# Pairwise bilinear products on one core: one ring of PSUM banks and multiplies of up to 2048 columns

## The chip, the cores and the metric

The kernel runs on one core of a Trainium2 chip. The metric is the device time of one execution in microseconds. The kernel before takes 1341.25 us (median of three executions, 1340.96 to 1341.39). The profiled execution has a span of 1339.7 us from its first to its last instruction.

## What is computed

The input x has 4096 rows of 32 fields with 64 numbers each, in float32. For each of the 496 pairs of fields (i, j) with i < j there is a 64 x 64 matrix W. The output for a pair is the row vector x_i times W, multiplied element by element with x_j:

```python
i_idx, j_idx = np.triu_indices(32, k=1)        # 496 pairs, i < j
vi = inputs[:, i_idx, :]                       # (4096, 496, 64)
vj = inputs[:, j_idx, :]
vdotw = jnp.einsum('bpd,pde->bpe', vi, W)
inter = vdotw * vj
return inter.reshape(B, -1)                    # (4096, 31744)
```

The output is 4096 x 31744 float32, 520 MB. Input x is 33.6 MB and W is 8.1 MB (8.4 MB with the zeros that the host adds).

## The kernel before

A row tile is 128 rows; there are 32. For a field i, all its products with later fields lie side by side in the output, (31 - i) x 64 columns wide. The kernel takes two fields at a time, 2p and 2p + 1, which it calls a pair p (16 of them): field 2p of x, transposed, lies on partitions 0 to 63 and field 2p + 1 on partitions 64 to 127, and so do their weights. The two halves of a pair differ by 64 columns in width; the host pads the weights of the second half with 64 zeros, so both have equal width in SBUF.

For each chunk of 512 columns, two matmuls (one per half) fill the two banks of one PSUM tile of 1024 columns, and VectorE multiplies the result with columns of x and writes it into a ring of 28160 columns in SBUF. When both halves of the chunk are 512 wide, one instruction multiplies both (1024 columns, read as two runs); the last chunk of a pair, where the halves differ, takes one instruction per half. PSUM has eight banks of 512 float32 columns; the kernel has them as four buffers of two banks.

```python
P = 128
BANK = 512
STORES = [[0, 1], [2, 3], [4, 5], [6, 7, 8], [9, 10, 11, 12, 13, 14, 15]]
PREFETCH_AT = [5, 6]
RING = 28160
...
psum = ctx.enter_context(tc.tile_pool(name="ps", bufs=4, space=bass.MemoryType.PSUM))
...
for t in range(NT):
    xt, xT = xs.pop(t), xTs.pop(t)
    if t + 1 < NT:
        xs[t + 1] = load_x(t + 1)
    for s, group in enumerate(STORES):
        ...                                    # osb: the next store_w[s] columns of the ring
        for p in group:
            if t + 1 < NT and p in PREFETCH_AT:
                ...
                transpose_x(xTs[t + 1], t + 1, xs[t + 1], PREFETCH_AT.index(p))
            for c0 in range(0, width[2 * p], BANK):
                pm = psum.tile([P, 2, BANK], F32, tag="ps", name=f"pm_{t}_{p}_{c0}")
                n = [max(0, min(BANK, width[2 * p + h] - c0)) for h in range(2)]
                for h in range(2):
                    if n[h]:
                        nc.tensor.matmul(pm[:, h, : n[h]],
                                         xT[h * D : (h + 1) * D, ts(p, P)],
                                         w_sb[p][h * D : (h + 1) * D, c0 : c0 + n[h]],
                                         start=True, stop=True)      # L120
                ...
                if n[0] == n[1]:
                    nc.vector.tensor_tensor(runs(osb, o[0], o[1], n[0]),
                                            pm[:, :, : n[0]],
                                            runs(xt, xj[0], xj[1], n[0]), ALU.mult)   # L130
                else:
                    for h in range(2):
                        if n[h]:
                            nc.vector.tensor_tensor(...)             # L139, one half each
        nc.sync.dma_start(out=out[ts(t, P), o0 : o0 + store_w[s]], in_=osb)   # L145
```

`transpose_x` takes one more PSUM buffer of the same four: eight 128 x 128 transposes on TensorE (L80), then a copy by ScalarE to SBUF (L81). It runs twice per row tile, ahead of pairs 5 and 6, for the next row tile. The pairs of one group in STORES are written to HBM with one transfer when the group is done; there are five such stores per row tile, of 2.75 to 3.78 MB (2752 to 3776 KB).

Of the kernel before, what the change touches and what calls it, by code (L numbers as in the profile page):

```python
# [1 line left out]

# [6 lines left out]

F32 = mybir.dt.float32  # L10
ALU = mybir.AluOpType

P = 128
BANK = 512

STORES = [[0, 1], [2, 3], [4, 5], [6, 7, 8], [9, 10, 11, 12, 13, 14, 15]]
PREFETCH_AT = [5, 6]
RING = 28160


@with_exitstack
def pair_bilinear_kernel(
    ctx: ExitStack,
    tc: tile.TileContext,
    x: bass.AP,
    w: bass.AP,
    out: bass.AP,
    F: int,
    D: int,
):  # L30

    nc = tc.nc
    B = x.shape[0]
    NT = B // P
    NPR = F // 2  # L50

    width = [(F - 1 - i) * D for i in range(F)]
    off = [sum(width[:i]) for i in range(F)]
    woff = [sum(width[0 : 2 * p : 2]) for p in range(NPR)]
    store_w = [sum(width[2 * p] + width[2 * p + 1] for p in g) for g in STORES]

    const = ctx.enter_context(tc.tile_pool(name="const", bufs=1))
    xpool = ctx.enter_context(tc.tile_pool(name="x", bufs=2))
    xtpool = ctx.enter_context(tc.tile_pool(name="xT", bufs=2))
    psum = ctx.enter_context(tc.tile_pool(name="ps", bufs=4, space=bass.MemoryType.PSUM))  # L60

    ident = const.tile([P, P], F32, tag="ident", name="ident")
    make_identity(nc, ident)

    def runs(tl, a, b, n):

        ap = tl[:, a : a + n]
        return bass.AP(ap.tensor, ap.offset, [list(ap.ap[0]), [b - a, 2], list(ap.ap[1])])

    def load_x(t):  # L70
        xt = xpool.tile([P, F * D], F32, tag="x", name=f"x_{t}")
        nc.scalar.dma_start(out=xt, in_=x[ts(t, P), :])
        return xt

    def transpose_x(xT, t, xt, g):

        n = 2 * BANK // P
        pt = psum.tile([P, 2 * BANK], F32, tag="ps", name=f"pt_{t}_{g}")
        for c in range(n):
            nc.tensor.transpose(pt[:, ts(c, P)], xt[:, ts(n * g + c, P)], ident)  # L80
        nc.scalar.copy(xT[:, ts(g, 2 * BANK)], pt)  # L81

    def new_xT(t):
        return xtpool.tile([P, NPR * P], F32, tag="xT", name=f"xT_{t}")

    ring = const.tile([P, RING], F32, tag="ring", name="ring")
    at = 0
    xs = {0: load_x(0)}

    w_sb = []  # L90
    for p in range(NPR):
        wp = const.tile([P, width[2 * p]], F32, tag=f"w{p}", name=f"w{p}")
        nc.sync.dma_start(out=wp, in_=w[:, woff[p] : woff[p] + width[2 * p]])
        w_sb.append(wp)

    xTs = {0: new_xT(0)}
    for g in range(2):
        transpose_x(xTs[0], 0, xs[0], g)
# [6 lines that stand above are left out]
            if at + store_w[s] > RING:  # L105
                at = 0
            osb = ring[:, at : at + store_w[s]]
            at += store_w[s]
            o0 = off[2 * group[0]]
            for p in group:  # L110
                if t + 1 < NT and p in PREFETCH_AT:
                    if t + 1 not in xTs:
                        xTs[t + 1] = new_xT(t + 1)
                    transpose_x(xTs[t + 1], t + 1, xs[t + 1], PREFETCH_AT.index(p))
                for c0 in range(0, width[2 * p], BANK):
                    pm = psum.tile([P, 2, BANK], F32, tag="ps", name=f"pm_{t}_{p}_{c0}")
                    n = [max(0, min(BANK, width[2 * p + h] - c0)) for h in range(2)]
                    for h in range(2):
                        if n[h]:
                            nc.tensor.matmul(  # L120
                                pm[:, h, : n[h]],
                                xT[h * D : (h + 1) * D, ts(p, P)],
                                w_sb[p][h * D : (h + 1) * D, c0 : c0 + n[h]],
                                start=True,
                                stop=True,
                            )
                    o = [off[2 * p + h] - o0 + c0 for h in range(2)]
                    xj = [(2 * p + h + 1) * D + c0 for h in range(2)]
                    if n[0] == n[1]:
                        nc.vector.tensor_tensor(  # L130
                            runs(osb, o[0], o[1], n[0]),
                            pm[:, :, : n[0]],
                            runs(xt, xj[0], xj[1], n[0]),
                            ALU.mult,
                        )
                    else:
                        for h in range(2):
                            if n[h]:
                                nc.vector.tensor_tensor(  # L139
                                    osb[:, o[h] : o[h] + n[h]],  # L140
                                    pm[:, h, : n[h]],
                                    xt[:, xj[h] : xj[h] + n[h]],
                                    ALU.mult,
                                )
            nc.sync.dma_start(out=out[ts(t, P), o0 : o0 + store_w[s]], in_=osb)  # L145


# [33 lines left out]
```

## Time and profile before

| what | value |
|---|---|
| time, median of three | 1341.25 us |
| span of the profiled execution | 1339.7 us |
| mean granted TensorE clock | 0.949 |
| HBM read / written | 41.94 MB / 520.09 MB |
| multiplies of 1024 columns (L130) | 768, mean 1217 ns |
| multiplies of one half, 64 to 448 columns (L139) | 896, mean 415 ns |
| matmul records of the products (L120) | 4864, mean 559 ns |
| transposes (L80), copies of them (L81) | 512, mean 297 ns; 64, mean 1012 ns |
| a store, from issue to landing | 22 to 23 us |

In the profile, PE is TensorE's matmuls, PEld its loads of weights (which overlap the matmuls), DVE is VectorE, ACT is ScalarE, SP issues the stores. A group of instructions is given as line, engine, operation, output<-input by the program's names (partitions x elements) and count, then the busy time in us and the mean duration in ns, then the time for which the engine stood idle before them and what ended that wait. Busy time is the time that a group covers; where two instructions overlap, it counts once, so it can be less than count times mean. In the row of slices, each digit is the busy share of a fortieth of the span in tenths, 9 being 90% or more. A line in the list of DMA queues has packets, megabytes, and the share of the 16 DMA engines' time. Matmuls are pipelined and their ends are modelled, so the busy share of PE does not say how near it is to its peak.

### The profile page before, as it was taken

The numbers are of one execution on the slowest core, as the hardware profiler recorded it, in microseconds if no ns is written. First come the engines' busy times: TensorE is split into PE (matmuls) and PEld (weight loads), VectorE is DVE, ScalarE is ACT, GpSimd is POOL, SyncE is SP. The second block draws the span as 40 slices with busy tenths as digits, with TensorE's granted clock in tenths as the row PEclk, the third lists the DMA queues.
The fourth block names the chain that finished last, engine by engine and source line by source line (L and its number), as shares of the span: only waits on it lengthen the run. The fifth ranks groups of instructions, "written<-read, shape, count | busy, mean of one in ns | idle before, by whom it ended". The sixth has DMA issues, their size and how long they took to land.

```text
span 1339.7 us, 13755 instructions
## 1 busy us (share of the span) xinstructions
PE 1151.0 (86%) x5376; PEld 548.7 (41%) x5376; DVE 1177.4 (88%) x1664; ACT 66.1 (5%) x65; POOL 0.7 (0%) x6
## 2 busy tenths in 40 slices
PE   7998889888898888988888978889798897888992
PEld 3444344443343443443433534444344443444441
DVE  6999889888899988989888989899898997898993
ACT  1000000000000000000000000000000000000000
POOL 0000000000000000000000000000000000000000
PEclk9999889999999999989999899899898998998996
DMA  9999999999999999999999999999999999999996
GB/s 392 426 431 434 429 431 429 427 427 434 426 434 430 422 422 430 422 424 429 415 426 424 426 426 404 415 420 431 428 420 408 431 427 431 416 424 420 422 429 264
DMA packets 30017, 562.93 MB, mean 420 GB/s; under 512 B 3456, under 2 KB 3840, under 8 KB 5376
## 3 DMA queue, kind: packets, MB, share of 16 engines
q1 hardware_dynamic: 25344, 528.49, 92.6%
q10 hardware_dynamic: 4608, 33.56, 6.0%
q8 instruction: 42, 0.69, 0.2%
q14 instruction: 23, 0.19, 0.0%
HBM read 41.94 MB, written 520.09 MB: 420 GB/s over the span
## 4 chain that ended last, share of the span: by engine, by line
DMA 54%; DVE 23%; PE 11%; issue 9%; DVEq 0%
DMA out_dram<-ring 54%; DVE ring L130 15%; PE pm L120 9%; DVE ring L139 9%; PE pt L80 2%; DMA x<-in_x_dram 1%; DVEq L130 0%; DVEq L177 0%
## 5 line engine op out<-in xcount | busy, mean ns | idle before, releaser
L120 PE MATMUL pm<-w,xT 64*128 64x512 f32 (+7 forms) x4864 | 1083.2, 559 | 158.3 <-DVE ring L130 140.1
L130 DVE TENSOR_TENSOR ring<-pm,x 128x1024 f32<-128x1024 f32 x768 | 904.0, 1217 | 138.4 <-DMA out_dram<-ring 93.0
L120 PEld LDWEIGHTS pm<-w,xT 64*128 64x128 f32 x4864 | 487.7, 194 | 720.1 <-DVE ring L130 451.3
L139 DVE TENSOR_TENSOR ring<-pm,x 128x448 f32<-128x448 f32 (+6 forms) x896 | 330.2, 415 | 3.6 <-PE pm L120 2.9
L81 ACT COPY xT<-pt 128x1024 f32<-128x1024 f32 x64 | 64.8, 1012 | 1194.6 <-PE pt L80 1194.6
L80 PE MATMUL pt<-ident,x 128*128 128x128 f32 x512 | 76.5, 297 | 8.5 <-DMA x<-in_x_dram 8.5
L80 PEld LDWEIGHTS pt<-ident,x 128*128 128x128 f32 x512 | 61.0, 152 | 48.9 <-issue 35.3
L81 ACT ACT_TABLE_LOAD x1 | 1.3, 1283 | 1.7 <-PEq L173 1.7
masks.py:199 POOL TENSOR_SCALAR_AFFINE_SELECT ident<-ident 128x128 f32<-128x128 f32 x1 | 0.3, 292 | 0.1
masks.py:197 POOL MEMSET ident<- 128x128 f32 x1 | 0.2, 204 | 0.3 <-POOLq L173 0.3
L173 POOL MEMSET const-bfloat16-1.0<- 128x1 bf16 x1 | 0.1, 101 | 0.0
L173 POOL MEMSET const-uint8-127<- 128x1 uint8 x1 | 0.1, 101 | 0.0
L173 POOL MEMSET const-float32-0.0<- 128x1 f32 x1 | 0.1, 98 | 0.2 <-issue 0.2
L173 POOL MEMSET const-float32-1.0<- 128x1 f32 x1 | 0.1, 98 | 0.0
## 6 DMA issues: line engine op xcount, KB each, us to landing
out_dram<-ring SPq DMA_DIRECT2D x32, 3776.0 KB, 22.8
out_dram<-ring SPq DMA_DIRECT2D x32, 3264.0 KB, 21.8
out_dram<-ring SPq DMA_DIRECT2D x32, 3168.0 KB, 22.4
out_dram<-ring SPq DMA_DIRECT2D x32, 2912.0 KB, 22.3
out_dram<-ring SPq DMA_DIRECT2D x32, 2752.0 KB, 22.1
x<-in_x_dram ACTq DMA_DIRECT2D x32, 1024.0 KB, 14.2
w<-in_w_dram SPq DMA_DIRECT2D x1, 992.0 KB, 7.4
w<-in_w_dram SPq DMA_DIRECT2D x1, 928.0 KB, 11.7
```

The costliest lines, as they stand in the source:

```text
L80: nc.tensor.transpose(pt[:, ts(c, P)], xt[:, ts(n * g + c, P)], ident)
L81: nc.scalar.copy(xT[:, ts(g, 2 * BANK)], pt)
L120: nc.tensor.matmul(pm[:, h, : n[h]], xT[h * D : (h + 1) * D, ts(p, P)], w_sb[p][h * D : (h + 1) * D, c0 : c0 + n[h]], start=True, stop=True,)
L130: nc.vector.tensor_tensor(runs(osb, o[0], o[1], n[0]), pm[:, :, : n[0]], runs(xt, xj[0], xj[1], n[0]), ALU.mult,)
L139: nc.vector.tensor_tensor(osb[:, o[h] : o[h] + n[h]], pm[:, h, : n[h]], xt[:, xj[h] : xj[h] + n[h]], ALU.mult,)
L173: nc = bacc.Bacc("TRN2", target_bir_lowering=False, num_devices=1)
```

## The change

PSUM becomes one tile of eight banks, and a small allocator hands out banks in turn; a request that doesn't fit before the end starts again at bank 0. A chunk is up to 1024 columns of each half: when the first half has more than 512 columns left, the chunk takes four banks, two per half, and otherwise two banks. One VectorE instruction multiplies both halves of a chunk, up to 2048 columns.

Unequal halves are also done in one instruction, both with the width of the first. The second half then gets 64 columns more than it has. The matmul fills them with zeros, because the weights there are zeros; the columns of x read for them run up to 64 columns past the end of a row, so x lies in two fixed buffers with 64 zero columns behind it; and the 64 products of zero are written beyond the pair's own place in the ring, where the next pair of the group writes its own values afterwards. That can't be done for the last pair of a group, nor where the second half doesn't reach into the chunk's last bank; those still take one instruction per half.

The purpose is fewer, longer VectorE instructions. The diff, with comments and blank lines left out:

```diff
+BANKS = 8
+CHUNK = 2 * BANK
...
-    xpool = ctx.enter_context(tc.tile_pool(name="x", bufs=2))
-    psum = ctx.enter_context(tc.tile_pool(name="ps", bufs=4, space=bass.MemoryType.PSUM))
+    psum = ctx.enter_context(tc.tile_pool(name="ps", bufs=1, space=bass.MemoryType.PSUM))
...
+    xbuf = [const.tile([P, (F + 1) * D], F32, tag=f"x{b}", name=f"x{b}") for b in range(2)]
+    for xb in xbuf:
+        nc.gpsimd.memset(xb[:, F * D :], 0.0)
...
+    pring = psum.tile([P, BANKS * BANK], F32, tag="pring", name="pring")
+    bank = 0
+    def take_banks(n):
+        nonlocal bank
+        if bank + n > BANKS:
+            bank = 0
+        got = pring[:, bank * BANK : (bank + n) * BANK]
+        bank = (bank + n) % BANKS
+        return got
...
-        pt = psum.tile([P, 2 * BANK], F32, tag="ps", name=f"pt_{t}_{g}")
+        pt = take_banks(2)
...
-                for c0 in range(0, width[2 * p], BANK):
-                    pm = psum.tile([P, 2, BANK], F32, tag="ps", name=f"pm_{t}_{p}_{c0}")
-                    n = [max(0, min(BANK, width[2 * p + h] - c0)) for h in range(2)]
-                    for h in range(2):
-                        if n[h]:
-                            nc.tensor.matmul(pm[:, h, : n[h]], ...)
+                for c0 in range(0, width[2 * p], CHUNK):
+                    n = [max(0, min(CHUNK, width[2 * p + h] - c0)) for h in range(2)]
+                    half = -(-n[0] // BANK) * BANK
+                    pm = take_banks(2 * half // BANK)
+                    for b0 in range(0, n[0], BANK):
+                        b1 = min(b0 + BANK, n[0])
+                        for h in range(2):
+                            if b0 < n[h]:
+                                nc.tensor.matmul(pm[:, h * half + b0 : h * half + b1], ...)
...
-                    if n[0] == n[1]:
+                    if n[1] > half - BANK and o[1] + n[0] <= store_w[s]:
                         nc.vector.tensor_tensor(
                             runs(osb, o[0], o[1], n[0]),
-                            pm[:, :, : n[0]],
+                            runs(pm, 0, half, n[0]),
                             runs(xt, xj[0], xj[1], n[0]),
                             ALU.mult,
                         )
```

More of the change, by code (lines that the diff above doesn't have):

```diff
@@ L68, in runs @@
         return bass.AP(ap.tensor, ap.offset, [list(ap.ap[0]), [b - a, 2], list(ap.ap[1])])
+    xbuf = [const.tile([P, (F + 1) * D], F32, tag=f"x{b}", name=f"x{b}") for b in range(2)]
+    for xb in xbuf:
+        nc.gpsimd.memset(xb[:, F * D :], 0.0)
     def load_x(t):
-        xt = xpool.tile([P, F * D], F32, tag="x", name=f"x_{t}")
-        nc.scalar.dma_start(out=xt, in_=x[ts(t, P), :])
-        return xt
+        xt = xbuf[t % 2]
+        nc.scalar.dma_start(out=xt[:, : F * D], in_=x[ts(t, P), :])
+        return xt
+    pring = psum.tile([P, BANKS * BANK], F32, tag="pring", name="pring")
[7 more added lines that the diff above has]
+        return got
     def transpose_x(xT, t, xt, g):
         n = 2 * BANK // P
-        pt = psum.tile([P, 2 * BANK], F32, tag="ps", name=f"pt_{t}_{g}")
+        pt = take_banks(2)
         for c in range(n):
@@ L114, in pair_bilinear_kernel @@
                     transpose_x(xTs[t + 1], t + 1, xs[t + 1], PREFETCH_AT.index(p))
-                for c0 in range(0, width[2 * p], BANK):
-                    pm = psum.tile([P, 2, BANK], F32, tag="ps", name=f"pm_{t}_{p}_{c0}")
-                    n = [max(0, min(BANK, width[2 * p + h] - c0)) for h in range(2)]
-                    for h in range(2):
-                        if n[h]:
[L120 to L126, printed above, removed]
+                for c0 in range(0, width[2 * p], CHUNK):
[6 more added lines that the diff above has]
+                            if b0 < n[h]:
+                                nc.tensor.matmul(
+                                    pm[:, h * half + b0 : h * half + b1],
+                                    xT[h * D : (h + 1) * D, ts(p, P)],
+                                    w_sb[p][h * D : (h + 1) * D, c0 + b0 : c0 + b1],
+                                    start=True,
+                                    stop=True,
+                                )
                     o = [off[2 * p + h] - o0 + c0 for h in range(2)]
                     xj = [(2 * p + h + 1) * D + c0 for h in range(2)]
-                    if n[0] == n[1]:
+                    if n[1] > half - BANK and o[1] + n[0] <= store_w[s]:
                         nc.vector.tensor_tensor(
                             runs(osb, o[0], o[1], n[0]),
-                            pm[:, :, : n[0]],
+                            runs(pm, 0, half, n[0]),
                             runs(xt, xj[0], xj[1], n[0]),
@@ L140, in pair_bilinear_kernel @@
                                     osb[:, o[h] : o[h] + n[h]],
-                                    pm[:, h, : n[h]],
+                                    pm[:, h * half : h * half + n[h]],
                                     xt[:, xj[h] : xj[h] + n[h]],
```

## The prediction

> **What bounds the kernel now.** I read the page's totals and its row of DMA shares first, then the groups by shape, then the waits of VectorE, and last the timeline of a few microseconds. The totals and the DMA part of the page:
>
> ```profile
> PE 1151.0 (86%) x5376; PEld 548.7 (41%) x5376; DVE 1177.4 (88%) x1664; ACT 66.1 (5%) x65; POOL 0.7 (0%) x6
> DMA  9999999999999999999999999999999999999996
> DMA packets 30017, 562.93 MB, mean 420 GB/s; under 512 B 3456, under 2 KB 3840, under 8 KB 5376
> q1 hardware_dynamic: 25344, 528.49, 92.6%
> q10 hardware_dynamic: 4608, 33.56, 6.0%
> ```
>
> Neither TensorE nor VectorE is full, but the transfers are: 92.6% for weights and stores plus 6.0% for the loads of x is 98.6% of the span, and no slice but the last falls under nine tenths. So the DMA engines set the pace: 0.986 x 1339.7 = 1321 us over 32 row tiles is **41.3 us a tile**. The waits say the same from the other side (engine, line waited for: total us, times, longest):
>
> ```profile
> DVE ring L130 <- DMA out_dram<-ring: 93.0, 53, 3.3
> DVE ring L130 <- PE pm L120: 45.4, 52, 13.2
> ```
>
> VectorE waits 93.0 us for space in the output ring, that is, for stores to land. For TensorE it waits 45.4 us, of which 13.2 is the start. Its time adds up: 1177.4 busy + 93.0 + 45.4 + 2.9 (the same wait at L139) = 1319 us, and its last multiply ends at 1319.5. Without the ring wait it would need (1177.4 + 32.2 + 2.9) / 32 = **37.9 us a tile**. So the producer has only 3.4 us a tile in hand.
>
> **What one multiply costs.** From the groups by shape:
>
> ```profile
> L130 DVE TENSOR_TENSOR ring<-pm,x 128x1024 f32<-128x1024 f32 x768 | 904.0, 1217 | 138.4 <-DMA out_dram<-ring 93.0 <-PE pm L120 45.4
> L139 DVE TENSOR_TENSOR ring<-pm,x 128x448 f32<-128x448 f32 x128 | 78.9, 617 | 3.6 <-PE pm L120 2.9
> L139 DVE TENSOR_TENSOR ring<-pm,x 128x64 f32<-128x64 f32 x128 | 27.6, 215 | 0.0
> ```
>
> (1217 - 617) / (1024 - 448) = 1.042 ns a column, or 960 columns a microsecond, and about 150 ns fixed. Back to back, neighbours overlap by some 0.085 us. What remains fixed is the busy time less the columns: 1177.4 / 32 = 36.79 us a tile, 31744 columns take 33.07, and 52 instructions share the other 3.72: **0.072 us each**.
>
> **What one refill of PSUM costs.** This decides my prediction. The timeline (start, length):
>
> ```profile
> 224.83 3.48 DVE L130 TENSOR_TENSOR ring<-pm,x 128x1024 f32<-128x1024 f32 x3
> 228.36 0.30 PEld L120 LDWEIGHTS pm<-w,xT 64*128 64x128 f32 x4 [0.83 <-DVE ring L130]
> ...
> 233.80 7.97 PE L120 MATMUL pm<-w,xT 64*128 64x512 f32 x38
> ...
> 234.34 0.19 PEld L120 LDWEIGHTS pm<-w,xT 64*128 64x128 f32 x2 [0.24 <-issue]
> 234.76 0.19 PEld L120 LDWEIGHTS pm<-w,xT 64*128 64x128 f32 x2 [0.23 <-issue]
> 234.98 2.36 DVE L130 TENSOR_TENSOR ring<-pm,x 128x1024 f32<-128x1024 f32 x2 [0.29 <-PE pm L120]
> ```
>
> A multiply ends at 224.83 + 3.48 = 228.31 and TensorE begins on the bank it freed at 228.36: 0.05 us. The lower lines show a multiply that waited: matmuls begin at 233.80, it starts at 234.98, **1.18 us** later, with two banks filled. The page counts 4864 matmul records, 152 a tile, where the loops call 76, so a call is two records. Loads of weights come in pairs every 0.43 us, so the two calls that fill two banks take 0.86 us, and 0.32 us is the way from matmul to multiply. Four banks then take 1.72 + 0.32 = 2.04 us, and from bank freed to multiply started it is **2.09 us**.
>
> [...]
>
> **The change, part by part.** *Multiplies.* Walking the loops, a tile goes from 52 multiplies over 31744 columns to 29 over 32320: nine unequal pairs are merged and each writes 64 extra zeros. 32320 / 960 + 29 x 0.072 = 33.67 + 2.09 = 35.75 us, so **1.0 us a tile is saved**. Since VectorE already waits 93 us for stores, this alone is hidden. *Matmuls* stay at 76 calls; transposes, loads, stores and bytes don't change. The two memsets at the start are outside the path.
>
> *Buffers.* Before: four slots of two banks, so TensorE may be three slots ahead. After: a chunk over 512 columns a half takes four banks, and only two such chunks fit. A refill can begin only when the multiply two chunks back has ended, and has one multiply as cover. A multiply of 2048 lasts 2.205 us in sequence and just covers 2.09. A short one doesn't. With the ring's order of banks worked out by hand, wrap included, the stall is 2.09 + 0.085 less the sequence time of the work between. In one tile:
>
> | chunk that stalls (columns) | work that covers it | its time | stall us |
> |---|---|---|---|
> | pair 0, first (2048) | pairs 14, 15: 384 + 64 | 0.61 | 1.56 |
> | pair 1, first (2048) | 1920 | 2.07 | 0.10 |
> | pair 2, first (2048) | 832 + 768 | 1.81 | 0.36 |
> | pair 3, first (2048) | 1408 | 1.54 | 0.64 |
> | pair 4, first (2048) | 576 + 512 | 1.28 | 0.90 |
> | pair 5, first (2048) | 896 | 1.00 | 1.17 |
> | pair 6, first (2048) | 320 + 256 | 0.74 | 1.43 |
> | pair 7, first (2048) | 384 | 0.47 | 1.70 |
> | pair 8 (1856, refill 1.98) | 64 | 0.14 | 1.93 |
>
> Pairs 6 to 8 stand in it because banks 6 and 7 are skipped when four no longer fit before the end, or hold a transpose. The later pairs find cover. The sum is **9.8 us a tile** in place of some 1.1 now. Then VectorE needs 35.75 + 9.8 = **45.5 us a tile**, more than the 41.3 of the DMA engines: the producer becomes the bound and the 93 us of ring waits vanish. The mean granted clock is 0.949; at that, nine refills of 1.72 us grow by 0.09 each and the tile takes 46.4.
>
> *The sum.* The first multiply starts at 13.16 now, and 0.86 later with four banks to fill: 14.0. Then 32 tiles: 1457 us at full clock, 1484 at 0.949, less 1.6 as the first tile has no tile before it. After the last multiply the program now takes 1339.7 - 1319.5 = 20.2 us; I keep 20. The measured time is 1.5 over the span. That is 14 + 1457 - 1.6 + 20 + 1.5 = 1491 us, or about 1518 at the lower clock. I take **1505 us**.
>
> **Rivals.** *Hidden by the transfers, 1341 us.* If refills overlapped better than my table has it, so that the stalls stay under 41.3 - 35.75 = 5.5 us a tile, the DMA engines stay the bound. For it: the full DMA row, and that TensorE's own work, 31 x 0.86 + 2 x 1.02 = 28.7 us a tile, is far under the limit. Against it: the table would have to be nearly twice too high, and its terms are seen in the trace. *The saving reaches the end.* If VectorE were the bound all along, 32 x 1.0 = 33 us go and 1308 us remain. The 93 us of ring waits and 420 GB/s speak against it. *A wait of VectorE on itself.* The 64 zeros that a merged multiply writes past its end are overwritten by the next pair's multiply; should that one be made to wait for the former's end, it loses the 0.085 us of overlap and some signalling, perhaps 0.12 us in six places a tile that no stall covers: 0.7 us a tile, 1528 us. Nothing in this trace shows whether it is made to wait.
>
> **Range and chances.** The low end takes a third off the stalls: 45.5 - 3.3 = 42.2 us a tile gives 1386, but a quarter off is as much as I believe, 43.1 or 1415. The high end is the lower clock with the wait on itself, 1541, and a little. So 1415 to 1545. Slower by over 2% gets 0.88, within 2% 0.09 for the hiding rival, faster 0.03.
>
> **What would show it.** VectorE's busy time falls from 1177 to about 1144 us with 928 multiplies. Its waits for TensorE rise from 48 to some 310 us in about nine places a tile, and its waits for stores fall from 93 to near zero. The DMA row loses its nines, with about 563 / 1.5 = 375 GB/s. A multiply that follows a lone 64-column one starts nearly 2 us late. If the waits for stores stay and the DMA row is full, the stall table is wrong and the first rival holds. A granted clock far from 0.949 would move the sum by some 27 us either way.

## The result, and the profile after

The changed kernel takes 1523.87 us (median, 1520.22 to 1526.17), the kernel before 1341.35 us measured beside it: a ratio of **1.136** (95% interval 1.134 to 1.138). The prediction was 1505 us in a range of 1415 to 1545.

The totals of the page after, with its rows for the TensorE clock and the transfers:

```profile
PE 1218.4 (80%) x5376; PEld 575.6 (38%) x5376; DVE 1176.2 (77%) x928; ACT 66.1 (4%) x65; POOL 0.9 (0%) x8
PEclk9999999999999999999999999999999999999998
DMA  9988898888988889888889888898888988889977
q1 hardware_dynamic: 25344, 528.49, 82.0%
```

The bytes are the same, but the DMA engines now have gaps in most slices: 82.0% in place of 92.6% for the stores and weights. VectorE runs 928 instructions in place of 1664 and is busy for as long as before. The waits after (engine, line waited for: us in total, times, longest):

```profile
DVE ring L155 <- PE pring L145: 239.5, 229, 15.2
DVE ring L164 <- PE pring L145: 83.5, 32, 3.5
```

No wait of VectorE for a store is left. It now waits for TensorE, 323 us in all, where before it was 48. The producer, TensorE and VectorE together, has become the bound. The timeline of VectorE shows where: the end of one row tile (pairs 7 to 10), then pairs 0 to 7 of the next (start, length; the number in brackets is the wait):

```profile
418.47 2.29 DVE L155 TENSOR_TENSOR ring<-pring,x 128x2048 f32<-128x2048 f32 x1 [1.63 <-PE pring L145]
420.68 0.21 DVE L164 TENSOR_TENSOR ring<-pring,x 128x64 f32<-128x64 f32 x1
422.73 2.16 DVE L164 TENSOR_TENSOR ring<-pring,x 128x960 f32<-128x960 f32 x2 [1.83 <-PE pring L145]
424.80 3.61 DVE L155 TENSOR_TENSOR ring<-pring,x 128x1664 f32<-128x1664 f32 x2
...
433.67 6.75 DVE L155 TENSOR_TENSOR ring<-pring,x 128x2048 f32<-128x2048 f32 x3 [1.08 <-PE pring L145]
440.34 1.88 DVE L164 TENSOR_TENSOR ring<-pring,x 128x832 f32<-128x832 f32 x2
442.51 3.82 DVE L155 TENSOR_TENSOR ring<-pring,x 128x2048 f32<-128x2048 f32 x2 [0.29 <-PE pring L145]
446.89 2.29 DVE L155 TENSOR_TENSOR ring<-pring,x 128x2048 f32<-128x2048 f32 x1 [0.56 <-PE pring L145]
...
451.27 3.29 DVE L155 TENSOR_TENSOR ring<-pring,x 128x2048 f32<-128x2048 f32 x2 [0.83 <-PE pring L145]
455.65 2.29 DVE L155 TENSOR_TENSOR ring<-pring,x 128x2048 f32<-128x2048 f32 x1 [1.09 <-PE pring L145]
457.86 0.81 DVE L164 TENSOR_TENSOR ring<-pring,x 128x320 f32<-128x320 f32 x2
460.04 2.76 DVE L155 TENSOR_TENSOR ring<-pring,x 128x2048 f32<-128x2048 f32 x2 [1.36 <-PE pring L145]
464.42 2.29 DVE L155 TENSOR_TENSOR ring<-pring,x 128x2048 f32<-128x2048 f32 x1 [1.62 <-PE pring L145]
```

Read it as a staircase. From pair 2 to pair 7 the wait ahead of the first chunk is 0.29, 0.56, 0.83, 1.09, 1.36 and 1.62 us; each cover, the second chunk of the pair before, takes 0.27 us less than the last (1.81, 1.54, 1.28, 1.00, 0.74 and 0.47 us in the prediction's table). Pair 8, covered only by 64 columns, waits 1.83. The table in the prediction had 0.36, 0.64, 0.90, 1.17, 1.43, 1.70 and 1.93, counted from where the multiply would have started with the usual overlap of 0.085 us; less that overlap the two agree within 0.02 us. These are waits at the full clock; what a lower clock adds is told below.

### The profile page after: what moved, and what is told of

The parts are those of the page before. It is cut to its first block, busy times and chain, and to the rows that moved or that the text cites. A ratio compares the mean times of both kernels' runs of the same rounds, so it can differ in the third digit from the quotient of the medians.

```text
span 1524.4 us, 12666 instructions
## 1 busy us (share of the span) xinstructions
PE 1218.4 (80%) x5376; PEld 575.6 (38%) x5376; DVE 1176.2 (77%) x928; ACT 66.1 (4%) x65; POOL 0.9 (0%) x8
## 4 chain that ended last, share of the span: by engine, by line
DVE 55%; PE 41%; issue 3%; DMA 0%; DVEq 0%
DVE ring L155 51%; PE pring L145 41%; DVE ring L164 4%; DMA x<-in_x_dram 0%; PE pring L102 0%; DVEq L155 0%; DVEq L164 0%
## 5 line engine op out<-in xcount | busy, mean ns | idle before, releaser
L145 PE MATMUL pring<-w,xT 64*128 64x512 f32 (+4 forms) x4864 | 1146.7, 559 | 286.2 <-DVE ring L155 277.0
L155 DVE TENSOR_TENSOR ring<-pring,x 128x2048 f32<-128x2048 f32 (+6 forms) x544 | 939.6, 1747 | 252.2 <-PE pring L145 239.5
L145 PEld LDWEIGHTS pring<-w,xT 64*128 64x128 f32 x4864 | 519.7, 192 | 893.2 <-DVE ring L155 462.5
L164 DVE TENSOR_TENSOR ring<-pring,x 128x64 f32<-128x64 f32 (+8 forms) x384 | 255.3, 700 | 86.8 <-PE pring L145 83.5
L103 ACT COPY xT<-pring 128x1024 f32<-128x1024 f32 x64 | 64.8, 1012 | 1377.7 <-PE pring L102 1336.7
L102 PE MATMUL pring<-ident,x 128*128 128x128 f32 x512 | 78.2, 287 | 8.4 <-DMA x<-in_x_dram 8.4
L102 PEld LDWEIGHTS pring<-ident,x 128*128 128x128 f32 x512 | 55.8, 143 | 44.3 <-issue 42.2
```

Of the source, the lines that this page charges most:

```text
L145: nc.tensor.matmul(pm[:, h * half + b0 : h * half + b1], xT[h * D : (h + 1) * D, ts(p, P)], w_sb[p][h * D : (h + 1) * D, c0 + b0 : c0 + b1 ...
L155: nc.vector.tensor_tensor(runs(osb, o[0], o[1], n[0]), runs(pm, 0, half, n[0]), runs(xt, xj[0], xj[1], n[0]), ALU.mult,)
L164: nc.vector.tensor_tensor(osb[:, o[h] : o[h] + n[h]], pm[:, h * half : h * half + n[h]], xt[:, xj[h] : xj[h] + n[h]], ALU.mult,)
```

## The experiments

**Two-bank chunks with everything else changed.** The merging of unequal halves and the ring of banks stay; only the chunk goes back to 512 columns a half.

```diff
-CHUNK = 2 * BANK
+CHUNK = BANK
```

> The changed kernel with chunks of 512 columns a half again, so every chunk takes two banks; the ring of banks and the merging of unequal halves stay. Theory (too few chunks fit in PSUM to cover a refill): a refill now has three chunks of cover, 43 multiplies take 32320 / 960 + 43 x 0.072 = 36.8 us a tile, some 1.7 more for the nine places where VectorE waits for itself and 1.1 for TensorE make 39.6, under the 41.3 of the DMA engines: 1341 us, and the waits for stores come back. Rival (the merging with its waits of VectorE on itself is the loss): the nine places are all still there, so the time stays near 1524. Rival (the ring of banks as one tile ties the engines together): also near 1524.

Measured: 1339.58 us, a ratio to the kernel before of 0.9988 (0.9982 to 0.9995). In its waits the stores are back, and TensorE is nearly gone (13.9 of the 32.0 us is the start):

```profile
DVE ring L155 <- DMA out_dram<-ring: 53.4, 35, 2.9
DVE ring L155 <- PE pring L145: 32.0, 29, 13.9
```

So neither the ring as one tile nor the merging is enough to make the kernel slower; what they may cost stays hidden under the transfers. The four-bank chunks are needed for the loss.

**Long chunks only where a long multiply covers them, and only where none does.** In both, the changed kernel's chunk depends on the pair:

```diff
-                for c0 in range(0, width[2 * p], CHUNK):
+                chunk = CHUNK if p < 4 else BANK              # second kernel: 4 <= p <= 8
+                for c0 in range(0, width[2 * p], chunk):
```

> The changed kernel with chunks of 1024 a half only in pairs 0 to 3, where a long multiply follows to cover the refill, and 512 a half from pair 4 on. Theory of PSUM cover: of the stalls in the table only those of pairs 0 to 3 remain, 1.1 + 0.1 + 0.4 + 0.6 = 2.2 us; 36.3 for the multiplies and some 1.5 for self-waits make 40 us a tile, just under the 41.3 of the DMA engines: 1341 to 1350 us. Rival (any multiply over four banks is slow, wherever it stands): four of the eight long ones remain, so about half the loss, 1430 us.

> The other half: chunks of 1024 a half only in pairs 4 to 8, where short multiplies follow, and 512 a half elsewhere. Theory of PSUM cover: the stalls of pairs 4 to 8 remain, about 0.9 + 1.2 + 1.4 + 1.7 + 1.9 = 7.1 us, 36.4 for the multiplies, some 1 for self-waits and 0.9 for the slow clock: 45 us a tile, 1470 us (1440 to 1510). Rival (any multiply over four banks is slow): half the loss, 1430 us, the same as with the early pairs.

Measured: 1339.06 us with the long chunks in pairs 0 to 3 (ratio 0.9984, 0.9977 to 0.9991), and 1424.17 us with them in pairs 4 to 8 (1.0619, 1.0603 to 1.0635). The waits of the first, then of the second:

```profile
DVE ring L156 <- PE pring L146: 86.3, 128, 13.9
DVE ring L156 <- DMA out_dram<-ring: 13.8, 18, 2.2
```

```profile
DVE ring L156 <- PE pring L146: 148.1, 131, 13.7
DVE ring L165 <- PE pring L146: 55.9, 32, 2.9
```

Taken alone, the 1424 us are below the theory's range and close to the rival's 1430. What decides is the pair of runs: the early pairs have eight four-bank chunks a row tile and the late ones five, yet only the late ones lose. So a multiply over four banks is not slow in itself. With the early pairs VectorE still waits for TensorE, 2.3 us a row tile without the start, (86.3 - 13.9) / 32, as the table had it (2.2); that fits under the time of the transfers, for which it goes on waiting. The late pairs cost less than expected, 43.7 us a row tile in place of 45: pair 7 waited 0.89 us instead of 1.62, because the trace has a multiply of 640 columns, of a later pair, between it and pair 6 (more on that below), pair 8 waited 1.71 instead of 1.83, and the clock stayed high (0.995).

**Fewer buffers, multiplies as they were.** The kernel before, with two buffers of two banks.

```diff
-    psum = ctx.enter_context(tc.tile_pool(name="ps", bufs=4, space=bass.MemoryType.PSUM))
+    psum = ctx.enter_context(tc.tile_pool(name="ps", bufs=2, space=bass.MemoryType.PSUM))
```

> The kernel before with two PSUM buffers of two banks in place of four; instructions, stores and loads are unchanged. Theory of PSUM cover: a refill of two banks takes 1.23 us and has one multiply of 1.14 or less as cover; the same table, chunk by chunk, gives 13.6 us of stalls a tile on 36.8 of multiplies: 50.4 us a tile, 13 + 32 x 50.4 + 10 = about 1640 us, with the multiplies as short as ever. Rival (it is the long multiplies that cost, not the number of buffers): 1341, as the DMA engines would still be the bound.

Measured: 1652.45 us, one run, where about 1640 was expected. Its row tiles take 51.0 us (31 periods between first multiplies), where the table worked out for it gave 50.4. The waits:

```profile
DVE ring L130 <- PE pm L120: 355.7, 418, 13.4
DVE ring L139 <- PE pm L120: 47.5, 51, 1.8
```

No instruction changed, and VectorE waits 403 us for TensorE. So fewer buffers in flight are enough for such a loss, and long multiplies are not needed for it.

**Half of the output not stored.** Each store writes only the first half of its columns, in the kernel before and in the changed one, so half of the output is left out and half of the store traffic is gone. The edit does a little more than that: a store no longer needs the multiplies of its second half, so it goes out earlier, and VectorE need not wait to overwrite that half.

```diff
-            nc.sync.dma_start(out=out[ts(t, P), o0 : o0 + store_w[s]], in_=osb)
+            nc.sync.dma_start(out=out[ts(t, P), o0 : o0 + store_w[s] // 2], in_=osb[:, : store_w[s] // 2])
```

> The kernel before, but each store writes only the first half of its columns: half of the output is left out, all multiplies stay. Theory (before, the DMA engines are the bound and VectorE has 3.4 us a tile in hand): the ring waits vanish and the time falls to VectorE's own 37.9 us a tile: 13 + 32 x 37.9 + 12 = 1238 us. Rival (VectorE or TensorE was the bound already): near 1341.

> The changed kernel, with the same half of the output left out. Theory (the producer is the bound, the transfers are not): the time stays at 1524, less 2 to 4 us as the last store is shorter. Rival (the transfers are still part of the loss, for instance because they run slower): it falls by 50 us or more.

Measured, one run each: 1194.73 us for the kernel before, where 1238 was expected, and 1512.28 us for the changed one. The totals of the first:

```profile
PE 1100.7 (92%) x5376; PEld 519.4 (44%) x5376; DVE 1168.4 (98%) x1664; ACT 66.1 (6%) x65; POOL 0.7 (0%) x6
```

VectorE is full at 98%. A row tile takes 36.81 us: 36.51 in which its 52 multiplies keep VectorE busy and one wait of 0.29 for TensorE. So the transfers were the bound before, and the producer had 4.5 us a tile in hand, not the 3.4 of the prediction. Of the 1.1 us of waits for TensorE that I had counted as its own, 0.29 remain. TensorE's clock is at 1.00 in this run and was 0.949 before; whether that is the reason is not shown.

The changed kernel loses only 12 us when half its stores go (14 between the two traced executions, with spans of 1524.4 and 1510.5 us). 7.7 of the 14 lie after the last multiply, 1.5 us in place of 9.2, where 2 to 4 were expected: the last store needs only pairs 9 and 10, and goes out 4.2 us before the last multiply ends. Row tiles take 46.66 in place of 46.85, which is 6 us over the run; up to the last multiply there are 17 stretches at half clock in place of 22. The first multiply starts 1 us earlier. The transfers are no longer the bound.

**Unequal halves not merged.** Chunks up to 1024 columns a half stay.

```diff
-                    if n[1] > half - BANK and o[1] + n[0] <= store_w[s]:
+                    if n[0] == n[1]:
```

> The changed kernel with chunks of up to 1024 columns a half, but unequal halves always take one multiply each, so no multiply writes past its place and none has to wait for the one before. Theory of PSUM cover: the nine refills stay uncovered; 31744 / 960 + 38 x 0.072 = 35.8 us a tile, 9.4 of stalls, no self-waits, and 0.9 for the slow stretches of TensorE's clock: 46.1 against 46.85 us a tile, 1500 us. Rival (self-waits and zeros are the loss): back to 1341 to 1380.

Measured: 1436.46 us (1.0713, 1.0697 to 1.0729). It lies between the two expectations, and neither has the size: long chunks without merging still cost 95 us over the kernel before, and the merging costs another 87 on top, not 24. The trace gives three parts of the 2.78 us a row tile (46.85 to 44.07). First the self-waits. Groups of the changed kernel by shape, then of this one:

```profile
L155 DVE TENSOR_TENSOR ring<-pring,x 128x640 f32<-128x640 f32 x32 | 26.4, 825 | 3.3
```

```profile
L164 DVE TENSOR_TENSOR ring<-pring,x 128x640 f32<-128x640 f32 x64 | 52.1, 815 | 0.0
```

In the changed kernel VectorE stands idle 3.3 / 32 = 0.10 us ahead of this multiply with no engine named. What the trace has there is a wait for a semaphore that VectorE's own multiplies raise; the multiply before it wrote zeros into its place. Without merging it starts 0.085 us before its neighbour ends. That is 0.19 us in each of four places (pairs 10, 13, 14 and 15), and 0.08 ahead of pair 1's first chunk: 0.8 us. Second, the clock: it stayed high here (0.997, no stretch at half clock before the last multiply), and in the changed kernel row tiles without such a stretch take 45.95 us, 0.9 under the mean. Third, about 1.1 us net, the order: with single halves the compiled program has moved multiplies of pairs 9 and 11 ahead, between the short ones of pairs 6 and 7. The timeline of VectorE shows it as three multiplies where pair 6 has two, and two where pair 7 has one:

```profile
616.28 1.41 DVE L164 TENSOR_TENSOR ring<-pring,x 128x192 f32<-128x192 f32 x3
618.45 2.29 DVE L155 TENSOR_TENSOR ring<-pring,x 128x2048 f32<-128x2048 f32 x1 [0.76 <-PE pring L145]
620.66 0.81 DVE L164 TENSOR_TENSOR ring<-pring,x 128x64 f32<-128x64 f32 x2
622.71 3.09 DVE L164 TENSOR_TENSOR ring<-pring,x 128x960 f32<-128x960 f32 x3 [1.24 <-PE pring L145]
```

The waits of pairs 7 and 8 fall from 1.62 and 1.83 to 0.76 and 1.24; 0.30 us come back as a wait in pair 10. More cover, less wait: the same mechanism again, from a side that the expectation had not thought of.

**Work for TensorE while it waits.** Redundant matmuls, overwritten by the real ones:

```diff
+                        if p in (6, 7) and c0:
+                            for h in range(2):
+                                if n[h]:
+                                    nc.tensor.matmul(pm[:, h * half : h * half + BANK], xT[...], w_sb[p][..., :BANK], ...)
```

> The changed kernel with redundant matmuls of 512 columns ahead of the second chunks of pairs 6 and 7, into the same banks, overwritten by the real ones; they fill time in which TensorE waits for a bank anyway. Theory (some 23 stretches of half clock, most of them at pair 8 after TensorE has been idle much, cost 0.9 us a tile of the loss): fewer such stretches and the tile goes from 46.85 towards the 45.95 of the tiles without one, 1495 to 1510 us. Rival (the half clock falls at fixed times or for another reason, or costs nothing): 1524, or later by the added matmuls, up to 1550.

Measured: 1498.78 us, 25 us less than the changed kernel (1.1175, 1.1157 to 1.1194, over the kernel before; the changed kernel had 1.1361). Pair 8's wait in the changed kernel, then here (by shape; the last two numbers are the idle time before it):

```profile
L164 DVE TENSOR_TENSOR ring<-pring,x 128x960 f32<-128x960 f32 x32 | 37.0, 1158 | 81.2 <-PE pring L145 81.2
```

```profile
L174 DVE TENSOR_TENSOR ring<-pring,x 128x960 f32<-128x960 f32 x32 | 37.0, 1157 | 56.9 <-PE pring L155 56.9
```

24 us come from this one place. What happens there is seen in the changed kernel's stretches around one pair 8 (busy us by engine, then the granted clock, DMA share and GB/s):

```profile
607.80:608.40 0.60, 0.54 (x2) 0.30 (x4) 0.14 (x2) 0.00 (x0) 0.00 (x0) 0.90 0.09 37
608.40:611.00 2.60, 2.60 (x9) 1.19 (x6) 0.00 (x0) 0.00 (x0) 0.00 (x0) 0.50 0.02 8
613.00:616.00 3.00, 2.65 (x11) 1.17 (x11) 2.90 (x3) 0.00 (x0) 0.00 (x0) 1.00 0.68 287
```

The refill of pair 8 runs at half clock; its multiply starts 3.2 us after the first matmul instead of 1.9. Before its last multiply the changed kernel has 22 stretches at 0.50, of 3.4 or 6.8 us, 92 us together. None of them follows a standstill of more than 1.9 us, TensorE's longest wait in this trace after the start.

```profile
PE pring L145 <- DVE ring L155: 277.0, 346, 1.9
```

With the extra matmuls there are 6 stretches, with 20 us, and the mean granted clock is 0.991 in place of 0.967. 20 of the 32 pairs 8 fell into such a stretch in the changed kernel, none with the extra matmuls: the longest wait ahead of a pair 8 was 3.5 us, and with them it is 1.8.

**The last store in three parts.** To the kernel with long chunks in pairs 0 to 3, which is 2 us under the kernel before:

```diff
+LAST = STORES[:-1] + [[9, 10], [11, 12], [13, 14, 15]]
...
-        for s, group in enumerate(STORES):
+        groups = LAST if t == NT - 1 else STORES
+        store_w = [sum(width[2 * p] + width[2 * p + 1] for p in g) for g in groups]
+        for s, group in enumerate(groups):
```

> The kernel with long chunks in pairs 0 to 3 only, and in the last row tile the group of pairs 9 to 15 is stored in three transfers in place of one, each when its pairs are done. In the last 20 us of the kernel before the DMA engines stand idle for about 3.3 us (0.07 x 10 + 0.07 x 5 + 0.45 x 5), because the last store of 2.75 MB can only start after the last multiply. Theory (the transfers are the bound everywhere else, so only such idle time can be won): 1 to 3 us less than the same kernel with one store, 1336 to 1338 us. Rival (the end is a fixed latency, not idle transfer time): 1339.

> The kernel with long chunks in pairs 0 to 3 only, once more beside the one with the last store split, on the same chip: 1339 us again, 0.1 to 0.2% under the kernel before.

Measured: 1339.48 us with the split (0.9986, 0.998 to 0.9993) and 1339.28 without (0.9984, 0.9978 to 0.9991). Nothing was won. The three smaller stores landed 18.8 to 19.3 us after they were issued, so they queued behind transfers already in hand, and the DMA engines are nearly full up to 1325 us either way (0.98 with the split and 0.93 without, from 1320 to 1325): most of what I had read as idle time looks like the queue running empty. (The last store is of 2912 KB, not of 2.75 MB.) The kernel with long early chunks is the fastest here, by 2 us or 0.16% under the kernel before. In the traces its last multiply ends 0.9 us earlier (1318.5 for 1319.5) and the time after that is 1.1 us shorter (19.1 for 20.3). Why stays open; the last pairs are not the reason, for from the last wait for a store to the last multiply it takes longer, 10.3 us for 9.3.

## Why the prediction was right, and which of its terms were off

The mechanism stood: two four-bank chunks leave one multiply as cover for a refill, short multiplies don't cover it, and the producer takes the place of the transfers as the bound. Two sides of it were tested: fewer buffers alone bring the loss, and shorter chunks alone take it away. The three rivals: hidden by the transfers and the saving reaching the end fell; the wait of VectorE on itself is real, 0.75 us a tile against my 0.7, but not in the central sum.

The terms of the sum, from the trace of the changed kernel:

| term | predicted | measured | difference over the run |
|---|---|---|---|
| first multiply starts | 14.0 | 15.2 | +1.2 |
| a row tile at full clock | 45.54 | 45.95 | +13 |
| half clock | 0 to 27 in all | 0.90 a tile | +29 on the full-clock sum |
| after the last multiply | 20 | 9.2 | -11 |

1491 + 1.2 + 13 + 29 - 11 = 1523. The traced execution took 1526.17 us; most of the other 3 us are the last row tile, which took 47.6 us, as two stretches at half clock fall into it. That the central 1505 missed by 19 us and not by 30 is luck: two terms were off in opposite directions.

*The row tile.* Pair 0's stall was put at 1.56 and is 1.08 + 0.085 = 1.17: its four banks come free in two steps, with the multiplies of pairs 12 and 13, and TensorE starts on the first two earlier. That is -0.4. The self-waits add 0.75, and pair 1's another 0.08.

*The clock.* I spread the mean clock of the kernel before, 0.949, over nine refills. The total was of the right size, but by luck, for the cause is another: the clock falls to a half in stretches, mostly at pair 8, and there it makes one refill longer, 3.2 us in place of 1.9. The first refill at the start is slow too: loads of weights come 0.85 us apart until 13.9 us and 0.43 later, hence the 1.2 us. (The record of the clock begins at 14.4 us.)

*The end.* I kept the 20 us that the kernel before takes after its last multiply. Most of that was a queue of stores: they land 22 to 23 us after their issue before and 9 to 12 after, where the transfers are not the bound. This term was simply wrong, by 11 us; it hid a third of what the clock added.

*VectorE's busy time.* 1144 us were expected and it is 1176. The 0.072 us that I took as an instruction's fixed cost is what remains when neighbours overlap; after a wait they don't, and the 0.085 us show up as busy time in nine or more places a tile. They were in my stalls, so the sum didn't change.

*The hand.* The producer of the kernel before needs 36.8 us a tile, not 37.9, as the run without half the stores shows.

## What to carry to other kernels

Before an instruction is made longer, count what it holds while it runs: with the eight banks of this kernel, doubling the chunk halves the chunks in flight, and each refill then has to be covered by the multiply beside it, so compare bank freed to consumer started (here 2.09 us for four banks) with the shortest piece of work that can stand there. Fewer instructions gained next to nothing here while the transfers were the bound (43 multiplies a tile in place of 52: a ratio of 0.9988), and can still lose the slack that kept them the bound (29 a tile: 1.136). Long chunks cost no time here where long work stands beside them, in pairs 0 to 3; choose the size per place, not for the whole loop.

## What was not expected of the hardware

In a kernel whose TensorE is busy 80% by the records and waits 1.9 us at most after the start, the clock dropped to a half 22 times, and that made the longest wait of the tile longer still, 3.05 us in place of 1.83 on average. Useless matmuls, 192 records more, made the kernel 25 us faster. What sets off a drop stays open. In the changed kernel each of the 22 follows 3.41 us, the length of the short stretches, in which matmuls were busy 44 to 54% of the time by the records; but nine other stretches of that length, at full clock and busy 47 to 52%, are followed by full clock again, so this share alone does not decide it.
